# Four layers of cross-attention and feed-forward: next keys behind the routing's choice, ternary weights fetched a region earlier, and a token-major feed-forward 3 with two chunks convolved on TensorE

## The chip, the cores and the metric

The kernel runs on one core of one Trainium2 chip. A core has five engines that run their own instruction streams side by side and wait for each other by semaphores: TensorE (PE, matrix multiply; its weight loads are listed as PEld), VectorE (DVE), ScalarE (ACT), GpSimd (POOL) and SyncE (SP, here a queue for DMAs). The metric is the device time of one execution in microseconds (us); lower is better.

## The reference, cut to what matters

The input is 8 sequences of 256 tokens of 256 values (2048 tokens). Each of four layers adds a gated cross-attention to a context of 256 tokens (16 heads of 16 values) and a gated feed-forward:

```python
for l in range(4):
    x = x + tanh(g_xattn[l]) * xattn[l](layernorm(x), ctx, ...)
    x = x + tanh(g_ffn[l]) * ffn[l](layernorm(x), ...)
```

Feed-forwards 1 and 2 route each token to the best two of eight experts (`top_k(logits, 2)`, then a softmax of the two weights). Feed-forward 3, in which most of the change lies, is:

```python
def act_quant(x):
    scale = 127.0 / clip(max(abs(x), axis=-1, keepdims=True), 1e-05)
    return clip(round(x * scale), -128, 127) / scale
def weight_quant(w):
    scale = 1.0 / clip(mean(abs(w)), 1e-05)
    return clip(round(w * scale), -1, 1) / scale
def bit_linear(x, w):
    return einsum('bsd,hd->bsh', act_quant(x), weight_quant(w))
h = bit_linear(x, w1)                   # 256 -> 1024
h = depthwise_conv1d(h, conv_w, conv_b) # 3 taps along the sequence
h = silu(h)
return bit_linear(h, w2)                # 1024 -> 256
```

So a token's 1024 hidden values need one common maximum before they are rounded, while the convolution runs over neighbouring tokens.

## The kernel before

Tokens lie in 16 tiles of 128 partitions; one batch element is two tiles. The work is emitted as "units", one for each head of each element (16 to an element), with hand-written offsets: `plan(at, f)` puts a piece of work behind unit `at`. Scores run 17 units ahead of the exponentials. A scheduler then orders the instructions of each engine; what goes through `pin` (all matmuls and turns, the exponentials) keeps the order in which it was written.

There are three regions with stages between them. Region 1 is attention 0 and 1 with feed-forward 0 and the routing of feed-forward 1; then the experts of feed-forward 1; region 2 is attention 2 with the routing of feed-forward 2; then its experts; region 3 is attention 3, with feed-forward 3 of an element following its attention.

An attention job projects queries, keys and values by TensorE (pq, pk, pv). `stack` splits queries or keys in three bf16 parts on POOL or DVE (L199 to L204), writes them to DRAM (L281) and reads them back as a stack on 112 partitions (L288), so that one bf16 matmul pair makes a head's scores (sc). DVE takes their negative maximum (L479), a second pair makes the transposed scores (st), ACT exponentiates (L523), `po` multiplies by the values; the turned sums (acc, DVE `o` L555, pm, ACT oT L571) go through py into x (L579).

`tail` puts the first work of the next region into the end of the current one: `early` holds `setup` (loads and the bias matmuls pgb) and keys and values of the next two jobs. Routing (`block`) of four tiles runs as norm, normT (pt_f), out (plf), choose and weigh on DVE, rank (two matmuls), place (DVE builds one-hot tables), tabulate (tabf). `slots` reads the table (tot, tok) and makes indices for indirect DMAs on POOL's queue; these gather tokens (xg) and expert weights (we) for 39 token tiles (L1036). Each tile is turned (ptg), multiplied (phg, gelu L1105, yg), scaled (ysb L1118) and written to yd. Later the `added` pieces of the next region gather the results and add them to x (L1158).

Feed-forward 3 takes two tiles at a time, hidden-major: partitions are hidden units, so eight chunks of 128x256 make up an element. `norm` normalizes (L169 is the power on POOL, L177) and scales by 127 over the maximum (L1248 to L1258), rounding by adding and subtracting the constant RND = 12582912. `normT` turns it on TensorE, and DVE takes RND off (L1264). `hidden(g)` makes two chunks: matmuls ph_f, DVE's multiplication by the scales into hp (L1284), the first tap with bias on ACT (L1294), the third on ACT into z (L1299), the second by DVE (L1301), and z's addition on POOL (L1306); the last element does taps two and three on DVE. Silu is one ACT instruction over 128x2048 (L1309). `largest` reduces the chunks per token on DVE with a strided view (L1316), `over` turns these maxima (pmx) to reduce over partitions, `spread` broadcasts the scales by TensorE (bc_yb) and ACT (L1338), `quantize(g)` multiplies and clips on POOL (L1343, L1344) and rounds on DVE (L1345). `out_` multiplies (y_f) and adds to x (L1357). Its weights are fetched in full precision (f3raw, 1 MB each, L1193) at the start of the second expert stage, summed (L1200) at its steps 8 and 16 and made ternary in quarters (L1220 to L1222).

Of the kernel before, what the change touches and what calls it, by code (L numbers as in the profile page):

```python
# [16 lines left out]
P = 128  # L17
# [21 lines left out]
def kernel(ctx: ExitStack, tc: tile.TileContext, a: dict, out: bass.AP):  # L39
# [183 lines left out]
    def attention(layers):  # L223
# [10 lines left out]
        def setup(l):  # L234
            y = lay[l] = {"bq": None, "bk": None}
            for n in "qkvo":
                w = awpool.tile([P, DC, D], F32, tag=f"w{n}", name=f"w{n}{l}")
                nc.sync.dma_start(w, a[f"L{l}_w{n}"].rearrange("(c p) o -> p c o", p=P))
                y[n] = w
            bv = None  # L240
            if l in (1, 3):
                y["bq"] = load(f"bq{l}", [P, DC], a[f"L{l}_bq"])
                nc.vector.tensor_scalar(y["bq"], y["bq"], 1.0 / DK**0.5, None, ALU.mult)
                y["bk"] = load(f"bk{l}", [P, DC], a[f"L{l}_bk"])
                bv = load(f"bv{l}", [P, DC], a[f"L{l}_bv"])


            bo = row(f"L{l}_bo")
            pb = bank(ps_m, "m", f"pgb{l}")[:, :D]
            if bv is not None:  # L250
                for c in range(DC):
                    bvb = keep.tile([P, P], F32, tag="bvb", name=f"bvb{l}_{c}", bufs=2)
                    nc.vector.tensor_copy(bvb, bv[:, c : c + 1].to_broadcast([P, P]))
                    mm(pb, bvb, y["o"][:, c, :], c == 0, False)
            mm(pb, ones[0:1, :], bo, bv is None, True)
            y["gb"] = keep.tile([P, D], F32, tag="gb", name=f"gb{l}")
            nc.vector.tensor_scalar(y["gb"], pb, tg[:, l : l + 1], None, ALU.mult)
# [38 lines left out]
        def prep(j, l, b):  # L296
# [96 lines left out]
            def proj(s, oc):  # L393

                if oc == 0:
                    o["p"] = bank(ps_m, "m", f"p{s}_{n}").rearrange("p (c s) -> p c s", c=DC)
                    o["t"] = keep.tile([P, DC, S], F32, tag=f"{s}T", name=f"{s}T_{n}")
                src = o["xs"] if s == "q" else ctxT[b]
                for c in range(DC):
                    mm(  # L400
                        o["p"][:, oc, :], lay[l][s][:, c, oc * P : (oc + 1) * P], src[:, c, :],
                        c == 0, c == DC - 1,
                    )
                bias = lay[l][f"b{s}"]
                scale = 1.0 / DK**0.5 if s == "q" else 1.0
                dst = o["t"][:, oc, :]
                if bias is not None:
                    nc.scalar.activation(  # L408
                        dst, o["p"][:, oc, :], AF.Identity, bias=bias[:, oc : oc + 1], scale=scale
                    )  # L410
                elif s == "q":
                    nc.scalar.mul(dst, o["p"][:, oc, :], scale)
                else:
                    nc.scalar.copy(dst, o["p"][:, oc, :])
                if s == "q" and lead and j == 0:

                    o["qs"] = stack(o["t"], s, j, oc, nc.vector)
                elif oc:
                    o[f"{s}s"] = stack(
                        o["t"], s, j, engine=nc.vector if s == "q" and lead and j == 1 else None  # L420
                    )
# [181 lines left out]
        for j, (l, b) in enumerate(jobs):  # L603
            if l and b == 0:
                if j:
                    plan(NH * (j - 2) - AHEAD - 6, setup, l)
                else:
                    early.append(lambda l=l: setup(l))
# [162 lines left out]
    def routing(l, pool, xd, gate, at0):  # L771
# [22 lines left out]
        def block(blk):  # L794
# [140 lines left out]
            def tabulate(h):  # L935
# [15 lines left out]
                (at + 22, out), (at + 23, choose), (at + 26, weigh), (at + 30, rank),  # L951
                (at + 32, lambda: place(0)), (at + 36, lambda: tabulate(0)),
                (at + 37, lambda: place(1)), (at + 41, lambda: tabulate(1)),
# [216 lines left out]
    def ffn3(home):  # L1170

        nh = 8
        w = {}
# [4 lines left out]
        def load_weights():  # L1178
            w["cw"] = load("cw", [P, nh, 3], a["L3_ffn_conv_w"])
            w["cb"] = load("cb", [P, nh], a["L3_ffn_conv_b"])  # L1180

        def ternary(n, at):
# [43 lines left out]
            return [(0, fetch), (at, total), (at + 1, mean)] + [  # L1226
# [13 lines left out]
        def element(pool, b):  # L1240
            n, o = f"f3_{b}", {}
            tiles = [2 * b, 2 * b + 1]

            def norm():

                xn = o["xn"] = normed(tiles, n)
# [7 lines left out]
                for i in range(2):  # L1254
                    nc.vector.tensor_scalar(
                        xn[:, i, :], xn[:, i, :], qs[:, i : i + 1], 127.0, ALU.mult, ALU.min
                    )
                nc.vector.tensor_scalar(xn, xn, -128.0, RND, ALU.max, ALU.add)  # L1258
                o["y"] = hbuf(f"h_{n}")
                o["q"] = pool.tile([P, nh, S], BF16, tag="f3qy", name=f"qy_{n}")  # L1260

            def normT():
                o["xqT"] = pool.tile([P, DC, S], BF16, tag="f3xT", name=f"xqT_{n}")
                nc.vector.tensor_scalar(  # L1264
                    o["xqT"], turn_pair(o["xn"], n), RND, None, ALU.subtract
                )
# [3 lines left out]
            def hidden(g):  # L1270
# [9 lines left out]

                hp = pool.tile([P, 2, S + 2], F32, tag="f3hp", name=f"hp_{n}_{g}")
                nc.gpsimd.memset(hp[:, :, 0:1], 0.0)
                nc.gpsimd.memset(hp[:, :, S + 1 : S + 2], 0.0)
                nc.vector.tensor_tensor(  # L1284
                    hp[:, :, 1 : S + 1], ph, o["dq"].to_broadcast([P, 2, S]), ALU.mult
                )
                cw = w["cw"]
                last = b == B - 1
                if not last:
                    z = pool.tile([P, 2, S], F32, tag="f3z", name=f"z_{n}_{g}", bufs=1)  # L1290
                for k in range(2):
# [6 lines left out]
                    if not last:  # L1298
                        nc.scalar.mul(z[:, k, :], hp[:, k, 2:], cw[:, hc, 2:3])  # L1299
                    for t in (1, 2) if last else (1,):  # L1300
# [3 lines left out]
                if not last:  # L1304
                    y = o["y"][:, 2 * g : 2 * g + 2, :]
                    nc.gpsimd.tensor_tensor(y, y, z, ALU.add)  # L1306

            def silu():
                pin(nc.scalar.activation(o["y"], o["y"], AF.Silu))  # L1309

            def largest():

                mx = pool.tile([P, S], F32, tag="f3mx", name=f"mx_{n}", bufs=1)
                pt = bank(ps_m, "m", f"pmx_{n}")[:, :S].rearrange("p (i s) -> p i s", i=2)
                for i in range(2):
                    nc.vector.tensor_reduce(  # L1316
                        mx[:, i * P : (i + 1) * P],
                        o["y"][:, :, i * P : (i + 1) * P].rearrange("p h s -> p s h"),
                        AX.X, ALU.max, apply_absolute_value=True,
                    )  # L1320
                o["mx"], o["pt"] = mx, pt

            def over():

                mx, pt = o["mx"], o["pt"]
                for i in range(2):
                    turn(pt[:, i, :], mx[:, i * P : (i + 1) * P], ident)
                ym = o["ym"] = small.tile([P, 2], F32, tag="ym", name=f"ym_{n}")
                nc.vector.tensor_reduce(ym, pt, AX.X, ALU.max)
# [6 lines left out]
            def spread():  # L1336
                o["yb"] = pool.tile([P, 1, S], F32, tag="f3yb", name=f"yb_{n}")
                nc.scalar.copy(o["yb"][:, 0, :], across(o["ysc"], f"yb_{n}"))  # L1338

            def quantize(g):  # L1340
                y = o["y"][:, 2 * g : 2 * g + 2, :]
                e = nc.vector if b == B - 1 and g % 2 else nc.gpsimd
                e.tensor_tensor(y, y, o["yb"].to_broadcast([P, 2, S]), ALU.mult)  # L1343
                e.tensor_scalar(y, y, 127.0, -128.0, ALU.min, ALU.max)  # L1344
                nc.vector.tensor_scalar(  # L1345
                    o["q"][:, 2 * g : 2 * g + 2, :], y, RND, RND, ALU.add, ALU.subtract
                )

            def out_(i):
# [14 lines left out]
                (12, norm), (15, normT), (31, silu), (33, largest), (35, over), (37, spread),  # L1364
            ]
            for g in range(nh // 2):
                plan += [
                    (17 + 2 * g, lambda g=g: hidden(g)), (39 + 2 * g, lambda g=g: quantize(g))
                ]
            plan += [(48 + i, lambda i=i: out_(i)) for i in range(2)]  # L1370
# [5 lines left out]
        return [(0, load_weights)] + ternary(1, 8) + ternary(2, 16), pieces  # L1376

    def moe(l, nh, nsets, apart, w, xd, between=(), scale=None):
        with tc.tile_pool(name=f"c{l}", bufs=1) as pool:
            with tc.tile_pool(name=f"rt{l}", bufs=1) as tmp:  # L1380
                rows = slots(l, pool, tmp, w, nsets)
            with tc.tile_pool(name=f"f{l}", bufs=1) as tiles:
# [4 lines left out]
    def tail(early, end):  # L1387

        at = [11, 12, 13, 14, 15, 23, 24, 25, 26]
# [7 lines left out]
    ahead = moe(1, 8, 3, True, w, xd[0])  # L1397
    early, run3 = attention((3,))
    with tc.tile_pool(name="r2", bufs=2) as pool:
        w, pieces = routing(2, pool, xd[1], tg[:, 6:7], 0)  # L1400
        run2(pool, pieces + tail(early, NH * B), ahead)
    with tc.tile_pool(name="f3w", bufs=1) as home:
        weights, pieces = ffn3(home)
        ahead = moe(2, 4, 5, False, w, xd[1], weights, w["nw"])
        with tc.tile_pool(name="r3", bufs=2) as pool:
            run3(pool, pieces(pool), ahead)
# [88 lines left out]
```

## Time and profile before

| what | value |
|---|---|
| runs | 1820.37 us median of 3 (1815.41 to 1821.47) |
| the profiled execution | 1816.64 us, of which the span is 1814.8 |
| mean granted TensorE clock | 0.898 |
| POOL busy | 679.9 us, 37% |
| region 1 | 0 to about 597 us |
| routing end and experts 1 | to about 922 us |
| region 2 | about 925 to 1190 us |
| routing end and experts 2 | to about 1390 us |
| region 3 with feed-forward 3 | 1390 to 1814.8 us |

The borders are read from the chain of work that ended last (the last `py` of a region, the last `ysb` or `yd` of an expert stage). In a group row the columns are line, engine, operation, output and input with their shapes, count, busy us and mean ns of one, then the engine's idle time before them. In a chain row they are the start, the length, the engine (or DMA), tensor and line, and how many instructions the piece holds. A float32 matmul is listed as two records, a turn as one. The groups of feed-forward 3 between 1475 and 1765 us that cost most outside TensorE:

```profile
L1306 POOL TENSOR_TENSOR h_f<-h_f,z_f 128x512 f32<-128x512 f32 x28 | 36.5, 1305 | 83.8 <-DVE h_f L1301 28.9 <-ACT pT L523 20.0 <-DVE ysc_f L1332 15.4
L1301 DVE SCALAR_TENSOR_TENSOR h_f<-hp_f,cw,h_f 128x256 f32<-128x256 f32 x56 | 35.0, 624 | 4.1 <-ACT h_f L1294 3.3
L1343 POOL TENSOR_TENSOR h_f<-h_f,yb_f 128x512 f32<-128x512 f32 x24 | 31.9, 1347 | 1.2 <-ACT yb_f L1338 0.4
L1316 DVE TENSOR_REDUCE mx_f<-h_f 128x128 f32<-128x1024 f32 x12 | 22.7, 1918 | 0.7 <-ACT h_f L1309 0.7
```

### The profile page before, as it was taken

To read this page: it belongs to the slowest core of one execution; us is meant where nothing else is said; L and a number is where in the kernel's file an instruction comes from. 1 tells how busy PE (TensorE), PEld (TensorE's weight loads), DVE (VectorE), ACT (ScalarE), POOL (GpSimd) and SP (SyncE) were. 2 spreads that over 40 slices of the span, in tenths; PEclk is the share of its full clock that TensorE was granted. 3 is DMA by queue.
4 is the path that set the end of the run, shared out by engine and by line. 5 is a ranking of instruction groups with operands and counts; after the bars stand their busy time and mean duration, and the time that the engine had idled before them with its cause. 6 is when DMAs were issued, how large, how long until landed. Compare 5 with 4: busy or idle time off the path is not lost.

```text
span 1814.8 us, 27468 instructions
## 1 busy us (share of the span) xinstructions
PE 1446.9 (80%) x9888; PEld 1097.3 (60%) x9918; DVE 946.7 (52%) x2918; ACT 742.2 (41%) x1629; POOL 679.9 (37%) x816
## 2 busy tenths in 40 slices
PE   1689888999998599999957888866997587776653
PEld 1356666676665399999944555546996454454432
DVE  4655554444767511111137767752422767778777
ACT  0354544555556133333314544512231256555641
POOL 2352232232330244343334453014553445554452
PEclk9899999999999799999978988977998788888876
DMA  6654222222541444242224535027341444222000
GB/s 165 150 152 99 69 60 59 60 60 59 129 131 30 112 150 138 88 135 85 85 71 111 132 96 140 17 78 244 99 149 56 129 100 102 66 56 57 7 6 18
DMA packets 101116, 170.11 MB, mean 94 GB/s; under 512 B 26642, under 2 KB 85141, under 8 KB 90197
## 3 DMA queue, kind: packets, MB, share of 16 engines
q1 hardware_dynamic: 71759, 113.93, 25.7%
q0 software_dynamic: 23664, 52.81, 8.9%
q10 hardware_dynamic: 5558, 1.63, 0.4%
q8 instruction: 78, 1.28, 0.3%
q14 instruction: 57, 0.47, 0.1%
HBM read 224.69 MB, written 41.68 MB: 147 GB/s over the span
## 4 chain that ended last, share of the span: by engine, by line
PE 59%; DVE 20%; DMA 8%; POOL 5%; issue 4%; ACT 3%; SPq 1%; ACTq 0%; POOLq 0%; DVEq 0%
PE phg L192 11%; PE yg L192 11%; PE po L192 5%; PE y_f L192 4%; PE st L192 4%; PE ph_f L192 4%; PE sc L192 4%; PE pv L192 3%; PE pk L192 3%; DVE nm L479 3%; PE pq L192 3%; DMA qstack<-mt 2%; DVE ms L474 2%; DMA kstack<-dr_k_None 1%; DMA xg<-xd,toki 1%
## 5 line engine op out<-in xcount | busy, mean ns | idle before, releaser
L523 ACT ACTIVATE pT<-st 128x512 f32<-128x512 f32 x512 | 298.9, 597 | 286.7 <-PE st L192 244.8
L479 DVE TENSOR_REDUCE nm<-sc 128x2 f32<-128x512 f32 x384 | 256.9, 681 | 119.7 <-PE sc L192 118.7
L192 PE MATMUL sc<-kstack,qstack 112*128 112x256 bf16 x1024 | 213.1, 297 | 95.5 <-DMA kstack<-dr_k_None 28.1
L1105 ACT ACTIVATE hg<-phg,we 128x128 f32<-128x128 f32 x468 | 133.5, 368 | 283.9 <-issue 259.6
L192 PE MATMUL st<-qstack,kstack 115*128 115x256 bf16 x1024 | 210.2, 290 | 44.3 <-ACT pT L523 23.6
L192 PEld LDWEIGHTS phg<-xgT,we 128*128 128x128 f32 x1872 | 224.3, 195 | 7.2 <-DVE xgT L1087 1.8
L192 PE MATMUL phg<-xgT,we 128*128 128x128 f32 x1872 | 225.8, 278 | 2.1 <-DVE xgT L1085 1.0
L192 PE MATMUL yg<-we,hg 128*128 128x256 f32 x936 | 214.6, 380 | 0.0
L192 PEld LDWEIGHTS <-qstack 112*128 112x128 bf16 x1024 | 101.7, 106 | 160.1 <-issue 120.9
L192 PEld LDWEIGHTS yg<-we,hg 128*128 128x128 f32 x936 | 172.2, 191 | 20.0
L192 PE MATMUL po<-pT,va 128*32 128x256 f32 x2048 | 155.0, 422 | 0.9
L192 PEld LDWEIGHTS <-kstack 115*128 115x128 bf16 x1024 | 105.0, 103 | 71.1 <-issue 37.3
L474 DVE CUSTOM_DVE_ANT_0 ms<-sc,mb 128x256 f32<-128x256 f32 x256 | 107.2, 419 | 70.2 <-PE sc L192 60.2
L1118 DVE TENSOR_TENSOR ysb<-yg,we 128x256 f32<-128x256 f32 x78 | 33.0, 424 | 169.3 <-PE yg L192 163.6
L169 POOL TENSOR_TENSOR rsr_ff<-rsv_ff,nhalf 128x4 f32<-128x4 f32 (+2 forms) x24 | 24.4, 1017 | 237.5 <-DVE rsv_ff L167 129.4
L192 PEld LDWEIGHTS po<-pT,va 128*32 128x32 f32 x2048 | 57.6, 117 | 64.3 <-issue 42.1
L1085 DVE COPY xgT<-ptg 128x256 f32<-128x256 f32 x39 | 16.5, 424 | 140.0 <-PE ptg L197 140.0
L1036 POOL DMA_INDIRECT xg<-xd,toki x78 | 74.7, 958 | 24.0 <-issue 23.2
L1036 POOL DMA_INDIRECT yg<-yd,rt_si x64 | 63.0, 984 | 51.4 <-issue 29.9
L1036 POOL DMA_INDIRECT we<-in_L_ffn_wa,wrow x39 | 38.8, 996 | 85.5 <-ACT hg L1105 73.0
L192 PE MATMUL ph_f<-xT_f,f0w 128*128 128x256 f32 x288 | 67.1, 390 | 2.8 <-DVE nm L479 2.0
L192 PE MATMUL pv<-wv,ctxT 128*128 128x256 f32 x192 | 59.7, 439 | 12.0 <-ACT kT L408 7.4
(254 smaller groups left out, 2516.3 us busy)
## 6 DMA issues: line engine op xcount, KB each, us to landing
kstack<-dr_k_None SPq DMA_DIRECT2D x160, 128.0 KB
qstack<-dr_q_None SPq DMA_DIRECT2D x60, 256.0 KB
dr_k_None<-pc_k SPq DMA_DIRECT2D x32, 384.0 KB
dr_q_None<-pc_q SPq DMA_DIRECT2D x30, 384.0 KB
qstack<-dr_q_None SPq DMA_DIRECT2D x30, 384.0 KB
yd<-ysb SPq DMA_DIRECT2D x78, 128.0 KB
kstack<-dr_k_None SPq DMA_DIRECT2D x32, 256.0 KB
xd<-fxn_f SPq DMA_DIRECT2D x8, 512.0 KB
```

The source lines that it names most:

```text
L169: pw = nc.gpsimd.tensor_tensor(rs, ve, nhalf[:, :k, :n], ALU.pow)
L192: pin(nc.tensor.matmul(out, lhsT=lhsT, rhs=rhs, start=start, stop=stop, skip_group_check=True))
L474: nc.vector.tensor_tensor_reduce(masked, sc[:, i, :], o["bias"][:, i, :], -1.0, 3.0e38, ALU.add, ALU.min, o["nm"][:, i, h : h + 1],)
L479: nm = nc.vector.tensor_reduce(o["nm"][:, :, h], sc, AX.X, ALU.max, negate=True)
L523: pin(nc.scalar.activation(pT[u], st, AF.Exp))
L1036: return nc.gpsimd.indirect_dma_start(out=dst, out_offset=None, in_=src, in_offset=bass.IndirectOffsetOnAxis(ap=rows, axis=0), **kw,)
L1085: nc.vector.tensor_copy(xT, pv)
L1105: nc.scalar.activation(h[:, hc, :], ph[:, k, :], AF.Gelu, bias=w[:, n1 - nh + hc : n1 - nh + hc + 1],)
L1118: nc.vector.tensor_tensor(ys, py, w[:, nh * D :], ALU.add)
```

## The change

**Tails.** `setup` keeps its loads; the bias matmuls become `bias`. In the tail only `setup`, `bias` and one job's keys and values remain, keys in two halves; the other job's run after `slots`, in the expert stage. Both jobs' key stacks of a later region are split on DVE.

**Routing.** The pieces from weigh on stand earlier by 2 to 7 units.

**Fetch.** The two 1 MB loads are planned in region 2, at the start of its seventh element. Sums, means and quarters keep their steps in the plan of the second expert stage.

**Feed-forward 3.** The statistics stand two units ahead of the norm; one DVE operation scales and adds RND, ACT takes RND off. hp has two fixed buffers. Chunks 0 and 1 are convolved on TensorE by three diagonal matrices each, and ACT evicts them with the bias. For the other chunks ACT does the first tap and DVE the other two. The chunks are then turned to token-major, ACT does silu while evicting, the maximum is a reduction along the row, and its scale a value per partition; DVE scales and adds RND, TensorE turns back, ACT takes RND off while evicting to bf16. Clipping is gone, as the scale bounds the values.

```diff
         def bias(l):
+            y = lay[l]
+            bo, bv = y["bo"], y["bv"]
             pb = bank(ps_m, "m", f"pgb{l}")[:, :D]
...
-                        o["t"], s, j, engine=nc.vector if s == "q" and lead and j == 1 else None
+                        o["t"], s, j, engine=nc.vector if lead and j == 1 else None
...
-                (at + 22, out), (at + 23, choose), (at + 26, weigh), (at + 30, rank),
-                (at + 32, lambda: place(0)), (at + 36, lambda: tabulate(0)),
-                (at + 37, lambda: place(1)), (at + 41, lambda: tabulate(1)),
+                (at + 22, out), (at + 23, choose), (at + 24, weigh), (at + 27, rank),
+                (at + 28, lambda: place(0)), (at + 31, lambda: tabulate(0)),
+                (at + 31, lambda: place(1)), (at + 34, lambda: tabulate(1)),
...
+            w["hp"] = [home.tile([P, 2, S + 2], F32, tag=f"f3hp{k}", name=f"hp_{k}") for k in range(2)]
...
+                        nc.vector.tensor_scalar(
+                            d[:, k, t, :], ident, cw[:, 2 * g + k, t : t + 1], None, ALU.mult
+                        )
...
-                nc.vector.tensor_scalar(xn, xn, -128.0, RND, ALU.max, ALU.add)
...
+            def whole(dst, src):
+                nc.scalar.activation(dst, src, AF.Identity, bias=w["nrnd"])
...
-                    if not last:
-                        nc.scalar.mul(z[:, k, :], hp[:, k, 2:], cw[:, hc, 2:3])
-                    for t in (1, 2) if last else (1,):
+                    for t in (1, 2):
                         nc.vector.scalar_tensor_tensor(
                             y, hp[:, k, t : t + S], cw[:, hc, t : t + 1], y, ALU.mult, ALU.add
                         )
-                if not last:
-                    y = o["y"][:, 2 * g : 2 * g + 2, :]
-                    nc.gpsimd.tensor_tensor(y, y, z, ALU.add)
+            def convolve(g):
...
+                        mm(
+                            pc[:, k, :], w["tap", g][:, k, t, :], hp[:, k, t : t + S],
+                            t == 0, t == 2,
+                        )
...
             def silu():
-                pin(nc.scalar.activation(o["y"], o["y"], AF.Silu))
+                for i in range(2):
+                    for h in range(2):
+                        py = bank(ps_m, "m", f"yt_{n}_{i}_{h}")
+                        for k in range(4):
+                            turn(
+                                py[:, k * P : (k + 1) * P],
+                                o["y"][:, 4 * h + k, i * P : (i + 1) * P], ident,
+                            )
+                        pin(nc.scalar.activation(
+                            o["yt"][:, i, h * BLK : (h + 1) * BLK], py, AF.Silu
+                        ))
...
-            def quantize(g):
-                y = o["y"][:, 2 * g : 2 * g + 2, :]
-                e = nc.vector if b == B - 1 and g % 2 else nc.gpsimd
-                e.tensor_tensor(y, y, o["yb"].to_broadcast([P, 2, S]), ALU.mult)
-                e.tensor_scalar(y, y, 127.0, -128.0, ALU.min, ALU.max)
+            def quantize(i):
+                y = o["yt"][:, i, :]
+                nc.vector.tensor_scalar(y, y, o["ysc"][:, i : i + 1], RND, ALU.mult, ALU.add)
+
+            def back(i, h):
...
+                    turn(pq[:, k * P : (k + 1) * P], o["yt"][:, i, hc * P : (hc + 1) * P], ident)
...
-                (12, norm), (15, normT), (31, silu), (33, largest), (35, over), (37, spread),
+                (11, measure), (13, norm), (15, normT), (31, silu), (33, largest),
+                (35, lambda: quantize(0)), (36, lambda: quantize(1)),
...
-            plan += [(48 + i, lambda i=i: out_(i)) for i in range(2)]
+            plan += [(37 + k, lambda k=k: back(*divmod(k, 2))) for k in range(4)]
+            plan += [(42 + i, lambda i=i: out_(i)) for i in range(2)]
...
                 rows = slots(l, pool, tmp, w, nsets)
+                for f in early:
+                    f()
...
-        at = [11, 12, 13, 14, 15, 23, 24, 25, 26]
+        at = [11, 24, 23, 24, 34, 38]
...
+            pieces += [(NH * (B - 2), f) for f in fetches]
```

## Prediction

> **What bounds the kernel now.** Four rows of the page come first: the engine sums, and the busy tenths of the span's 40 slices (45.4 us each).
>
> ```profile
> PE 1446.9 (80%) x9888; PEld 1097.3 (60%) x9918; DVE 946.7 (52%) x2918; ACT 742.2 (41%) x1629; POOL 679.9 (37%) x816
> PE   1689888999998599999957888866997587776653
> DVE  4655554444767511111137767752422767778777
> PEclk9899999999999799999978988977998788888876
> ```
>
> TensorE is full only in the expert stages (slices 15 to 20 and 27 to 30). From slice 33 on, which is attention layer 3 with feed-forward 3, neither PE nor DVE is full and the granted clock sinks. The window table says so in us (engine, busy, instructions; then clock):
>
> ```profile
> core 0: us, PE busy (x) PEld busy (x) DVE busy (x) ACT busy (x) POOL busy (x), PEclk, DMA share, GB/s
> 1300.00:1390.00 90.00, 89.72 (x618) 84.26 (x617) 24.78 (x63) 27.44 (x96) 40.49 (x42) 1.00 0.34 107
> 1420.00:1765.00 345.00, 244.35 (x1664) 160.46 (x1663) 262.13 (x581) 191.92 (x364) 169.64 (x227) 0.84 0.26 63
> 1765.00:1815.00 50.00, 17.91 (x84) 11.11 (x84) 36.69 (x65) 7.39 (x12) 14.20 (x17) 0.64 0.05 16
> ```
>
> The experts are pure TensorE. Region 3 (1420 to 1765) has PE 71%, DVE 76%, POOL 49% at clock 0.84: waits passed from engine to engine bound it. The chain of waits through one element (start, length, what) shows them:
>
> ```profile
> 1556.14 2.32 DVE x L1158 x2
> ...
> 1564.75 1.76 POOL x L373 x2
> ...
> 1568.39 0.71 POOL rsr_ff L169
> ...
> 1572.60 1.10 PE pt_f L197 x4
> ...
> 1594.35 0.59 PE acc L197 x4
> ...
> 1595.87 2.51 POOL h_f L1343 x2
> 1598.45 0.62 POOL h_f L1344
> ...
> 1603.62 2.32 DVE x L1158 x2
> ```
>
> Equal points lie 1603.62 − 1556.14 = **47.5 us** apart: one element. The PE pieces of this chain and of the ones beside it, taken where they run at full clock (sc and st 0.22 a pair, po 1.00, py, pk, pv and pq about 2.0, ph_f and y_f 1.76), add up to 27.2 us an element. The wait view gives PE 12.5 us idle in 1556 to 1603: 3.1 for the norm (DVE L1258, which waited for POOL's power L169, itself queued behind L373), 2.8 for DVE `o`, because DVE stood at L1345 waiting for POOL's quantize, 2.3 for ACT, 1.7 for kT, the rest small. The remaining 7.8 us is the half-rate clock after idle: four turns cost 1.10 us at 1572.6 and 0.59 at 1594.
>
> The routing tail, here tail 2, by the chain:
>
> ```profile
> 1205.61 0.66 PE pt_f L197 x4
> 1206.27 1.95 PE plf L192 x16
> ...
> 1211.50 1.72 PE pv L192 x4
> ...
> 1214.80 0.38 PE rankf L192 x4
> ...
> 1226.64 0.62 POOL we L1036
> ...
> 1228.04 10.49 DMA xg<-xd,toki
> ```
>
> Keys and values of the next region stand on PE ahead of `plf` and of `rank`; the first gather then takes 10.49 us (4.75 in tail 1, chain at 630.27), with the two 1 MB ternary weights in front.
>
> **Feed-forward 3, one element.** POOL loses L1306 (4 × 1.31), L1343 (4 × 1.35), L1344 (4 × 0.68) and 8 memsets of 0.1: 14.1 us, at once or by contention. DVE loses 8 L1301 of 0.62 (5.0), 2 L1316 of 1.92 (3.8), 4 L1345 of 0.66 (2.6), L1264 (0.69), L1258 (0.43); it gains 12 STTs (0.48, the median of all L1301: 5.8), two reduces over 128x1024 (half of L1200's 2.28: 1.14 each) and two in-place scalings of 1024 (twice L1221's 0.42: 0.83 each). L1255 stays. −12.5 + 9.7 = −2.8 us. Besides, L1158 takes 1.16 us each beside POOL's quantize and 0.47 to 0.5 elsewhere (0.50 at 932.6), so −1.3. ACT loses 8 z of 0.50, two first terms of 0.59, the 1.91 silu and the 0.38 copy (7.5) and gains 4 silus, 4 evictions and xqT at about 0.59 and two 128x256 evictions at about 0.4 (6.1): −1.4; the table load stays one pair an element in after's order.
>
> PE gains six float32 taps of 128x256 at 0.5 (py: two such in 1.0 to 1.13) = 3.0, and 32 turns; it loses bc_yb 0.46 and pmx 0.22. The acc row of the chain, four turns in 0.59, gives 0.15 a turn: 4.8 us. Against the change speaks the Trainium skill, "TensorE: Matmul & The Clock Gate", Part 4: a turn took about 275 ns in a kernel, and turns don't count as PE work for the clock. By that rule 32 turns are 8.8 us, 4.0 an element or 25 over 6.2 elements more. The trace has both prices, 1.10/4 = 0.275 after an idle and 0.15 in a busy stream; the new turns come in two groups of 16 inside region 3's stream, so I take the 0.15 and keep the 0.275 for the range. PE: 27.2 − 0.7 + 7.8 = **34.3 us**.
>
> Idle: `measure` two steps ahead takes the power off the path (−3.1), no quantize on POOL (−2.8), shorter adds (about −1.5 of 2.3): 12.5 becomes 5.1. New: the first turn for the silu waits for ACT's and DVE's last chunk, and `back` for the DVE scaling: 1 to 2 us, less when other units fill it; I take 1.5. The 7.8 of slow clock should fall with the idle to about 2. Sum 34.3 + 5.1 + 1.5 + 2 ≈ **43 us**, −4.5. What is late next is DVE (36.35 − 4.1 ≈ 32 of 43) and nm L479 behind the scaling. Bounds: 39.5 (idle falls to 4, clock recovers) and 47.5. The feed-forward runs from 1475 to 1765, 290/47 = 6.2 periods: **−28 us** (−50 to 0).
>
> The last element's end, 1793.7 to 1814.8, is 21.1 us: silu 1.9, maxima 3.7, spread 3, POOL 3.4, DVE, y_f. After: 16 turns with 4 silus behind them 4.5, two maxima 2.3, small ones 0.9, two scalings 1.6 partly beside turns, turns and evictions 3, y_f and add 2: 14.3. **−7** (−4 to −9).
>
> **Routing tails.** After's order on PE is pt_f, plf, half of pk, pgb, the other half, rank; later the table matmuls, one v, and only then tot and tok. In tail 2 plf at 1206.27 stands behind 11.2 us of PE (pgb, pk, pv from 1193.95), but its operand is ready only about 1199: plf at 1200 to 1202, choose (3.7 in tail 2, 1208.2 to 1211.9) to 1205.7, while PE does pk and pgb for 2.0 + 3.2 + 2.1 us: rank at about 1209.3 in place of 1214.80, −5.5. The first block's earlier rank and place bring 1, the v ahead of the token matmuls costs 2.2 (full clock) to 3.6 (half), 3 taken: first gather 3.5 us earlier. The other job's k and v and its k stack now fall among the gathers. The stack's DMAs fill all engines for 6.3 us (0.38 MB written, 0.9 MB read); by "DMA: Bandwidth & Descriptors" of the skill (arbitration) an engine alternates between queue rows, so a gather of 4.75 us is at most doubled, while by the row 10.49 it waits for all that is ahead. I take +3, bounds 0 and +6. The ternary fetch gone from there is worth 10.49 − 4.75 = −5.7. Tail 2: −3.5 + 3 − 5.7 ≈ **−6** (−3 to −11). Tail 1, at a faster clock: rank from 616.66 to about 610.5, first block −1, v +3, so −4 for the gathers; the k stack +5, since all three first tiles came at 420 GB/s and landed at 646.8, with no fetch to take away: **+1** (−4 to +3).
>
> **The fetch in region 2.** Planned at unit 96, it has no predecessor, and after's instruction order has both 1 MB loads on SP at region 2's very start, six tap builds (128x128, about 0.3) on DVE before the first adds, and the two totals of 2.28 us inside the first query split. Queued behind a total: pc_q, dr_q, the query stack, the first scores (949.13). Loads: 2 MB at the 420 GB/s of the gathers of tail 1 are 5 us, at 925 to 931, beside the yg gathers (landed 932.5): +1.5 (0 to +4). Totals 4.6, of which DVE's idle before (it waited 2.09 for pq) covers 2.5; taps lie in the wait for yd: **+3** together (0 to +7). Means and quarters are DVE work under a full PE, as before.
>
> Sum against the profiled execution (1816.6; span 1814.8): −28 − 7 − 6 + 1 + 3 = −37, **1780 us**. The median of the three runs shown lies 4 us above that execution, inside their own spread of 6; I leave it out.
>
> **Rivals.**
> - Given back (0.19): DMA at the two entries costs its upper bounds (+7, +3, tail 2 −3) and the period only falls to 44.5: 1816.6 − 19 + 7 + 3 − 3 − 7 ≈ 1798. For: tail 2's 10.49. Against: tail 1's third tile landed only at 646.8 anyway.
> - More (0.14): POOL's absence speeds all DVE rows (L1301 mean 0.66, median 0.48), period 39.5: 1816.6 − 50 − 7 − 6 + 4 ≈ 1757.
> - Slower (0.10): TensorE bounds region 3. Its 7.1 us more an element come on top of idles that only move, with turns at half rate. The rest of the change gives 9 us, 1.5 a period, so it decides from the point where less than 5.6 of the 20.3 us idle and slow clock go away. If 3 go: 51.6 a period, 4.1 × 6.2 = +25, −9: 1833. For: PE's pieces grow by a quarter and clock is 0.84. Against: 5.9 of the idle has a named cause that is removed.
> - No effect (0.05): the same mechanism at about 5.6 us: 1817.
>
> The likeliest (0.52) is 1766 to 1793 by itself. The range, 1745 to 1807, leaves out the slower case and the tail of the fast one. About 0.3% (5 us) is what a measurement tells from no change: faster 0.85, within 0.05, slower 0.10.
>
> **What would show it.** POOL nearly empty in region 3 but for splits, powers and adds; L1158's successor near 0.5 us; period 43 with PE busy above 80% and clock near 0.9; turns 0.15 each; rank right after choose, gathers of tail 2 some 3.5 us earlier; first scores of region 2 about 3 us later; a first gather of tail 2 well under 10.49. It is wrong if PE's idle for DVE stays near 12 us, or if the turns run in 0.275.

## The result and the profile after

The changed kernel takes 1795.9 us (median of 4, 1787.15 to 1800.92) where the kernel before took 1819.11; the ratio is 0.9877, 95% interval 0.9847 to 0.9908. It is faster by 1.2%, inside the forecast's range, by about 23 us instead of 37. The same rows of the page, and the window table over region 3 up to the last attention output, and from there to the end:

```profile
PE 1483.7 (83%) x10192; PEld 1135.7 (63%) x10222; DVE 911.7 (51%) x2913; ACT 742.5 (41%) x1629; POOL 573.0 (32%) x660
PE   1589988999999689999966887876999378888876
DVE  4655554454667611111117678754332557766865
PEclk9799999999999799999986999877999689888998
```

```profile
core 0: us, PE busy (x) PEld busy (x) DVE busy (x) ACT busy (x) POOL busy (x), PEclk, DMA share, GB/s
1420.00:1755.00 335.00, 269.68 (x1923) 189.58 (x1924) 232.56 (x578) 186.36 (x351) 85.80 (x99) 0.90 0.27 67
1755.00:1794.00 39.00, 25.11 (x148) 18.60 (x145) 22.32 (x53) 14.78 (x26) 0.70 (x1) 0.86 0.06 21
```

POOL has lost half its work in region 3 (170 to 86 us), DVE 30 us, TensorE has gained 25 us, and its clock went from 0.84 to 0.90. That is the forecast's picture. But a sum hides what happened. The table below cuts the span of each profile at the same events, read from the timelines: the last attention output added to x in a region (py), the first token matmul (tok), a tile's first turn (ptg), the last ysb, and the fourth gathered result added (yg). Each entry is the time since the row above, in us. The last three columns are experiments told below.

| up to | before | changed | feed-forward 3 alone | tails alone | values behind slots |
|---|---|---|---|---|---|
| last py, region 1 | 600.5 | 598.0 | 597.5 | 603.8 | 596.7 |
| tok, tail 1 | 25.5 | 29.7 | 25.6 | 29.9 | 25.7 |
| third tile's ptg | 20.9 | 23.1 | 21.0 | 22.8 | 22.3 |
| last ysb, experts 1 | 275.6 | 275.6 | 275.6 | 276.1 | 277.3 |
| fourth yg | 10.5 | 13.0 | 12.9 | 9.8 | 13.4 |
| last py, region 2 | 258.6 | 256.9 | 259.1 | 255.0 | 255.6 |
| tok, tail 2 | 32.5 | 33.9 | 31.9 | 34.2 | 30.0 |
| first tile's ptg | 14.5 | 9.1 | 8.9 | 9.1 | 9.6 |
| last ysb, experts 2 | 151.5 | 155.2 | 150.4 | 168.0 | 152.2 |
| fourth yg | 10.0 | 9.9 | 9.8 | 9.9 | 9.9 |
| py of element 0, region 3 | 80.5 | 82.6 | 80.1 | 80.6 | 79.8 |
| py of element 3 | 131.2 | 130.0 | 125.0 | 130.7 | 127.8 |
| py of element 7 | 152.7 | 138.3 | 138.7 | 152.7 | 137.3 |
| end | 50.3 | 39.1 | 38.3 | 50.4 | 38.3 |

Region 3 (the last four rows) fell from 414.7 to 390.0 us; everything ahead of it rose by 4.4. The forecast had −35 and −2. A row holds one execution of each kernel: region 1, which the change hardly touches, differs by 2.5 us. In both tails the token matmul, which was to come about 4 us earlier, came later. The chain of waits in tail 1 of the changed kernel shows how:

```profile
600.48 1.41 PE pt_f L197 x8
601.91 3.38 PE plf L192 x16
605.30 1.91 PE pk L192 x4
607.20 1.15 PE pgb L192 x2
608.35 2.02 PE pk L192 x4
...
610.90 0.56 DVE rt_c L892
611.67 1.02 DVE rtf_run L878
...
619.55 0.52 PE tabf L192 x2
620.07 1.83 PE pv L192 x4
621.92 0.38 ACT va L435
622.34 2.07 PE pv L192 x4
624.42 0.24 PE tot L192 x2
```

`plf` starts 5.0 us earlier than before (606.91), of which 2.5 are region 1's, and the gain is lost step by step. TensorE was idle for 3.0 us until 600.48 and has a granted clock of 0.52 from there to 636: plf takes 3.38 us where it took 1.95. Then DVE's choose takes from 605.3 to 614.6 where it took 3.7: it holds an instruction that waits for pgb (1.52 us of idle in the DVE timeline) and weigh's first step, which waits for ACT's exponential (1.03). Two of the four run sums L878 take 1.10 and 1.13 us for 8 values each while POOL splits a key stack. (The change moved only the second job's key stack to DVE, at 633.27; the first job's is still split on POOL, from 610.83.) Last, both halves of a value projection and an eviction between them, 4.3 us, stand between the last table and `tot`. In tail 2 rank does come early, 18.2 us behind the last py in place of 23.1; there two DVE steps behind it take 1.17 us each beside POOL's split (0.17 and 0.34 otherwise), and the value with its eviction takes 4.2.

In region 3 the chain of the element from 1569 to 1617 us shows another loss:

```profile
1574.97 0.94 PE pq L192 x4
...
1576.49 1.28 ACT L1358
1577.78 0.61 ACT yt_f L1358
...
1578.43 1.13 PE yt_f L197 x4
...
1579.58 0.61 ACT yt_f L1358
...
1580.23 1.13 PE yt_f L197 x4
...
1581.38 0.61 ACT yt_f L1358
...
1582.03 1.13 PE yt_f L197 x4
...
1583.83 1.13 PE pt_f L197 x4
```

The four groups of turns ahead of the silu and the four evictions go strictly one after the other. ACT's 1.28 us at 1576.49 load the silu's table. Three of the groups take 1.13 us: 0.28 a turn, the price of the half-rate clock (0.50 granted from 1578.4 to 1592). The PSUM pool has two banks, but half of the query projection stands at 1574.97 and its second half comes only behind the turns, so its bank stays open and the turns have one. Behind the silu ACT also evicts the next element's norm before it loads the table of the exponentials again:

```profile
1576.49 1.28 ACT L1358 ACT_TABLE_LOAD   x1
1587.37 1.28 ACT L527 ACT_TABLE_LOAD   x1
```

So 10.9 us pass from one load to the other without an exponential; in the same place of the kernel before they are 6.1 (1570.04 to 1576.12).

### The profile page after: what moved, and what is told of

It is laid out like the page before. It is cut to its first block, busy times and chain, and to the rows that moved or that the text cites. A ratio compares the mean times of both kernels' runs of the same rounds, so it can differ in the third digit from the quotient of the medians.

```text
span 1794.6 us, 27891 instructions
## 1 busy us (share of the span) xinstructions
PE 1483.7 (83%) x10192; PEld 1135.7 (63%) x10222; DVE 911.7 (51%) x2913; ACT 742.5 (41%) x1629; POOL 573.0 (32%) x660
## 4 chain that ended last, share of the span: by engine, by line
PE 58%; DVE 18%; issue 8%; DMA 7%; POOL 4%; ACT 3%; SPq 0%; POOLq 0%; ACTq 0%; DVEq 0%
PE yg L192 11%; PE phg L192 11%; PE po L192 5%; PE ph_f L192 4%; PE y_f L192 4%; PE st L192 4%; PE sc L192 4%; DVE nm L483 3%; PE pk L192 3%; PE pq L192 2%; PE pv L192 2%; DMA xg<-xd,toki 2%; DMA kstack<-dr_k_None 2%; DVE ms L478 1%; DMA qstack<-mt 1%
## 5 line engine op out<-in xcount | busy, mean ns | idle before, releaser
L192 PE MATMUL sc<-kstack,qstack 112*128 112x256 bf16 x1024 | 208.8, 292 | 100.2 <-DMA kstack<-dr_k_None 32.2
L192 PE MATMUL st<-qstack,kstack 115*128 115x256 bf16 x1024 | 205.2, 284 | 19.2 <-DMA qstack<-mt 15.7
L192 PE MATMUL po<-pT,va 128*32 128x256 f32 x2048 | 150.8, 416 | 0.9
L169 POOL TENSOR_TENSOR rsr_ff<-rsv_ff,nhalf 128x4 f32<-128x4 f32 (+2 forms) x24 | 24.4, 1015 | 327.5 <-DVE rsv_ff L163 188.0
L1041 POOL DMA_INDIRECT yg<-yd,rt_si x64 | 63.4, 991 | 51.4 <-issue 29.7
L169 POOL TENSOR_TENSOR rsr_a<-rsv_a,nhalf 128x2 f32<-128x2 f32 x32 | 23.5, 738 | 147.2 <-DVE rsv_a L163 146.8
L192 PE MATMUL pq<-xs,wq 128*128 128x256 f32 x192 | 65.3, 472 | 4.4 <-ACT qT L412 1.9
```

Of the source, the lines that this page charges most:

```text
L169: pw = nc.gpsimd.tensor_tensor(rs, ve, nhalf[:, :k, :n], ALU.pow)
L192: pin(nc.tensor.matmul(out, lhsT=lhsT, rhs=rhs, start=start, stop=stop, skip_group_check=True))
L1041: return nc.gpsimd.indirect_dma_start(out=dst, out_offset=None, in_=src, in_offset=bass.IndirectOffsetOnAxis(ap=rows, axis=0), **kw,)
```

## The experiments

**Feed-forward 3 alone.** The changed kernel with the tails, the routing offsets and the fetch's planned place of before:

```diff
-                (at + 22, out), (at + 23, choose), (at + 24, weigh), (at + 27, rank),
+                (at + 22, out), (at + 23, choose), (at + 26, weigh), (at + 30, rank),
...
-        at = [11, 24, 23, 24, 34, 38]
+        at = [11, 11, 12, 13, 14, 15, 23, 24, 25, 26]
...
-    ahead = moe(1, 8, 3, True, w, xd[0], early[6:])
+    ahead = moe(1, 8, 3, True, w, xd[0], [])
...
```

> Feed-forward 3 of the changed kernel alone; tails, routing offsets and the fetch as before. Theory A (region 3 gains about 25 us, the entries of regions 2 and 3 together give back about 4): 1794 less 4, about 1790 us, with first x addition of region 3 at 1399.6 as before and about 24 us less from there to the end. Rival B (the tails and the fetch help, as forecast, by about 12 us in the full change): 1805 us or more.

Measured: 1776.28 us, ratio 0.9772 (0.9721 to 0.9822), below even theory A. Region 3 falls by 32.6 us (table), and the yg gathers and the first tile of the second experts come as in the changed kernel, since the loads still went out at region 2's start (see below). Of the 40.0 us between the two profiles 3.0 lie in region 1, which feed-forward 3 doesn't touch.

**Tails alone**, on the kernel before: the split of setup, the routing offsets, the new places, the second job's keys and values behind the slots and its key stack on DVE.

> Tails and routing offsets of the changed kernel alone; fetch and feed-forward 3 as before. Theory A (value projections ahead of the token matmuls and key stacks among the gathers cost more than the earlier rank brings): slower than before by 4 to 10 us, last ysb of the first experts at about 926 in place of 922.2. Rival B (the forecast's sum of the tails without the fetch, +1 and about 0): within 2 us of before.

Measured: 1840.07 us, ratio 1.0115 (1.0072 to 1.0158): slower by 20 us, twice theory A's upper end. The changed kernel lies 19.6 us above feed-forward 3 alone, so the tails cost about 20 us in both surroundings, though not in the same places: the second experts take 168.0 us here, 16.5 more than before, and in the changed kernel 4.8 more than with feed-forward 3 alone. The wait view of TensorE in that stage (us in total, times, longest), and DVE's timeline there (in brackets the idle time and its cause):

```profile
PE phg L192 <- DVE xgT L1093: 9.1, 3, 8.4
PE yg L192 <- DVE ysb L1124: 3.1, 1, 3.1
PE phg L192 <- issue: 3.0, 1, 3.0
```

```profile
1260.75 2.29 DVE L1206 TENSOR_REDUCE wab<-f3raw 128x1 f32<-128x2048 f32 x1 [8.98 <-DMA f3raw<-in_L_ffn_w]
1262.95 0.41 DVE L1093 TENSOR_TENSOR xgT<-ptg,nw 128x256 f32<-128x256 f32 x1
```

DVE's sum over the first raw weight waits 9 us for its load, whose issue on SP (1241.77) stands behind the second job's key stack, and the next tile's eviction (xgT) stands behind the sum.

**Fetch put back**, in the changed kernel's plan.

```diff
-            fetches.append(fetch)
-            return [(at, total), (at + 1, mean)] + [
+            return [(0, fetch), (at, total), (at + 1, mean)] + [
```

> The changed kernel with the two 1 MB ternary loads put back at the start of the second expert stage. Theory A (the loads at region 2's start cost there 5 to 6 us, through the yg gathers and two totals, of which most is hidden later by region 2's slack; in tail 2 they cost about 5.7): between 0 and 6 us slower than the changed kernel, first scores of region 2 at about 951 and first gathered tile of the second experts some 5 us later. Rival B (the early loads only cost): faster than the changed kernel by 4 us or more.

Measured: 1802.17 us (1786.2 to 1806.92), 0.99 (0.9854 to 0.9946), not separable from the changed kernel. And its edit moved nothing: SP issues both loads at 929.03, against 929.19 in the changed kernel. The load waits for no one, so it goes out where its buffers exist, and they are opened before region 2. What moves the fetch is the pool, not the plan. Neither theory was tested. The version serves as a second measurement of practically the same instruction order: its median lies 6.3 us from the changed kernel's and its region 3 takes 382.7 us in place of 390.0, elements 1 to 3 of it 125.2 in place of 130.0. Smaller differences between two medians or two profiles show nothing by themselves.

**Fetch really late**: feed-forward 3 alone, with the pool opened behind region 2 (loads at 1208.58 and 1212.04).

```diff
-    with tc.tile_pool(name="f3w", bufs=1) as home:
-        fetches, weights, pieces3 = ffn3(home)
-        with tc.tile_pool(name="r2", bufs=2) as pool:
+    with tc.tile_pool(name="r2", bufs=2) as pool:
...
+    with tc.tile_pool(name="f3w", bufs=1) as home:
+        fetches, weights, pieces3 = ffn3(home)
```

> Feed-forward 3 alone, its buffers opened only behind region 2, so that the two ternary loads go out with the second experts' first gathers as before. Theory A (the early loads cost about 2.5 us at the yg gathers of region 2 and save about 5.5 before the second experts' first tile): 2 to 5 us above feed-forward 3 alone, first tile of the second experts 14.5 us behind the token matmul in place of 9. Rival B (the place of the loads does not matter once slack is counted): within 1 us.

Measured: 1782.81 us (1772.02 to 1786.4), against 1776.28 (1773.42 to 1784.5): the ranges overlap. In the profile the fourth yg came after 10.7 us in place of 12.9, the first tile of the second experts after 13.6 in place of 8.9: −2.2 and +4.7, as theory A has them, though the total doesn't prove it. (Tails alone reach 9.1 us at that first tile too, without an early fetch: their loads stand behind the key stack on SP and go out at 1241.77, behind the first gathers, where the kernel before has them at 1220.79.)

**Tails alone with the early pool**, to see what the fetch does for the tails.

> Tails and routing offsets alone, with the ternary buffers opened before region 2, so that the two 1 MB loads go out at its start. Theory A (in the tails-alone kernel DVE's sum over the first raw weight waits for a load queued behind the second job's key stack, and holds the next tile's turn for TensorE): the waits of 8.4 and 3 us in the second experts go, that stage takes 152 to 160 us in place of 168, 1825 us. Rival B (the key stacks' own DMAs make the stage long): within 4 us of tails alone, 1840.

Measured: 1833.51 us (1824.68 to 1841.66, 15 runs), 1.0071 (1.005 to 1.0092). The second experts take 156.9 us in place of 168.0, as theory A had it. The total fell by less, 6.6 us; against tails alone in the profile, yg took 3.0 us and region 2 another 7.4 us more (region 2 differs by as much among the other profiles). So the early fetch repairs the stall in the experts that the tails make, and the tails stay slower than before.

**Values behind the slots**: the changed kernel, with the last two places taken out of the tail.

```diff
-        at = [11, 24, 23, 24, 34, 38]
+        at = [11, 24, 23, 24]
...
-    ahead = moe(1, 8, 3, True, w, xd[0], early[6:])
+    ahead = moe(1, 8, 3, True, w, xd[0], early[4:])
...
```

> The changed kernel with both value projections of the first job taken out of the tail too and placed behind the slots, with the second job's. Theory A (each tail loses the 4.2 us that two value halves stand ahead of the token matmuls): first token matmul 25.5 us after the last py of region 1 in place of 29.7, the same in tail 2, 5 to 9 us faster than the changed kernel, about 1788 us. Rival B (the key stacks' DMAs decide when the third tile lands): within 3 us of the changed kernel.

Measured: 1777.78 us (1777.3 to 1785.64), 0.9779 (0.9735 to 0.9823): 18 us below the changed kernel, with intervals apart. The token matmuls come 4.0 and 3.9 us earlier, as theory A says; the second experts take 3.0 us less; the rest is spread over region 2's end and region 3 in the two single profiles, and what carries it there isn't settled. This one placement is the cost of the new tails: without it they equal the old ones (1776.28). The rows name 11 of its 18 us.

**Silu one unit later**, behind the second half of the query projection, with all that follows it; first in the changed kernel, then in feed-forward 3 alone.

```diff
-                (11, measure), (13, norm), (15, normT), (31, silu), (33, largest),
-                (35, lambda: quantize(0)), (36, lambda: quantize(1)),
+                (11, measure), (13, norm), (15, normT), (32, silu), (34, largest),
+                (36, lambda: quantize(0)), (37, lambda: quantize(1)),
...
```

> The changed kernel with silu and all pieces behind it one unit later, so that the query projection has closed its PSUM bank before the turns. Theory A (the four groups of turns go through one bank, one after the other, because the other is held open by a half-done query projection): in the three elements concerned the waits of yt for ACT fall from 3.5 us to under 1.5 and the elements get 3 to 5 us shorter, 9 to 14 us in all: about 1784 us. Rival B (the turns wait for ACT anyway, or DVE decides): within 3 us of the changed kernel.

> Feed-forward 3 alone (tails and routing as before), with silu and what follows one unit later. Theory A (free second PSUM bank for the turns): 5 to 10 us below feed-forward 3 alone, 1766 to 1771 us. Rival B (the gain of the first such run lies in the tails): within 3 us of feed-forward 3 alone, 1776.

Measured: 1790.99 us, 4.9 below the changed kernel, and 1771.54, 4.7 below feed-forward 3 alone; each pair's ranges overlap, and two measurements of one order lay 6.3 us apart, so the totals alone don't show a gain; both go the same way by the same amount. One element of feed-forward 3 alone, first as it is, then with the later silu, each in its window and its wait of the turns for ACT (us in total, times, longest):

```profile
1551.00:1597.00 46.00, 37.47 (x263) 26.49 (x261) 31.45 (x82) 26.28 (x49) 13.48 (x17) 0.89 0.31 76
```

```profile
PE yt_f L197 <- ACT yt_f L1357: 3.5, 3, 2.1
```

```profile
1556.00:1597.00 41.00, 34.38 (x265) 24.74 (x265) 31.64 (x82) 25.88 (x49) 14.29 (x17) 1.00 0.33 85
```

```profile
PE yt_f L197 <- ACT yt_f L1357: 1.3, 1, 1.3
```

The wait falls to 1.3 us and the granted clock rises to 1.00, as theory A says; elements 1 to 3 take 116.6 us in place of 125.0. With the early silu they took 125.0 to 130.0 in five profiles, with the late one 116.6 and 120.4, so this gain stands. Whether the free bank alone makes it isn't shown, because the edit also moves the silu behind the next element's norm, whose evictions stood between the silu and the exponentials. The two table loads of this element now lie 3.7 us apart:

```profile
1567.48 1.28 ACT L1357 ACT_TABLE_LOAD   x1
1571.22 1.28 ACT L527 ACT_TABLE_LOAD   x1
```

But the last stretch grows from 38.3 to 40.8, and the sum stays below what was expected: behind the last attention a later silu is only late.

**No convolution on TensorE**, feed-forward 3 alone.

```diff
-        TAPS = (0,), (0,)
+        TAPS = (), ()
```

> Feed-forward 3 alone with no chunk convolved on TensorE: all eight chunks go through ACT and two DVE operations. Theory A (DVE and ACT are nearer the limit than TensorE): 3 to 10 us above feed-forward 3 alone, mostly in the last element. Rival B (TensorE is the bound, the six taps of 0.5 us cost 3 us an element): 5 to 15 us below it.

Measured: 1765.07 us (1757.35 to 1774.74), 0.9704 (0.9647 to 0.9761), 11 us below feed-forward 3 alone, as rival B says, though the intervals overlap (0.9721 was the other's lower end). The gain is 3.1 us in elements 1 to 3, 8.9 in 4 to 7 and 4.4 at the end. The second of these elements, 1597 to 1641 us with taps and 1597 to 1637 without:

```profile
1597.00:1641.00 44.00, 36.55 (x266) 26.27 (x265) 30.12 (x74) 26.39 (x49) 9.94 (x12) 0.92 0.28 67
```

```profile
1597.00:1637.00 40.00, 30.97 (x247) 21.81 (x246) 32.62 (x77) 26.11 (x49) 9.48 (x11) 1.00 0.32 74
```

TensorE works 5.6 us less, of which the taps are about 3 and the rest goes with the higher clock; DVE works 2.5 more, and the element is 4 us shorter.

**Combinations.** Both edits on feed-forward 3 alone; both on the whole change with values behind the slots; and the last with the keys behind rank, the bias later and weigh planned behind rank (`at = [11, 35, 28, 30]`, weigh at 29).

> Feed-forward 3 alone on the tails and routing of before, without the TensorE convolution and with silu one unit later. Theory A (both gains are TensorE time and add up: 11 and 5 us below 1776): about 1760 us. Rival B (without taps the silu's bank matters less): 1765 us, as without taps alone.

> The whole changed kernel with value projections behind the slots, no TensorE convolution and silu one unit later. Theory A (the same two gains on top of 1778): about 1762 us, equal to the version with the old tails within 4 us. Rival B (key stacks among the gathers still cost): 5 us or more above it.

> As the last, and in the tail the first job's keys behind rank instead of ahead of it, the bias behind the keys, weigh planned behind rank. Theory A (rank waited for two key halves and the bias, choose for the bias and for the softmax's exponential): token matmul 21 to 23 us behind the last py in place of 25.6, in both tails, so about 6 us below the last: 1755 us. Rival B (half-rate clock eats it): within 3 us of the last.

Measured: 1780.35 us (0.9775, 0.9734 to 0.9816), 1776.02 (0.9755, 0.9709 to 0.9802) and 1786.68 (0.9816, 0.9772 to 0.986). The gains don't add up, and without the taps the later silu's version is 8.8 us slower than with them (1771.54). The kernel before took 1820.1 us on the chip of one of these two and 1821.4 on that of the other, so the chip is hardly the reason. With the later silu the version without taps takes 138.0 us for elements 4 to 7 and 40.9 at the end, where it had 129.8 and 33.9; in elements 1 to 3 it gains nothing in this profile (122.4 against 121.9), though the next version, with the same code there, took 117.6. Elements 1 to 7 of four versions: feed-forward 3 alone, the same without taps, with the later silu, and with both:

```profile
1472.80:1736.50 263.70, 215.41 (x1586) 152.87 (x1584) 187.78 (x475) 158.54 (x297) 53.13 (x62) 0.93 0.22 53
1474.80:1726.60 251.80, 196.17 (x1502) 136.88 (x1500) 203.96 (x503) 158.93 (x297) 53.84 (x62) 0.93 0.23 56
1479.90:1732.50 252.60, 206.24 (x1586) 145.69 (x1584) 187.70 (x476) 156.97 (x297) 54.39 (x62) 0.98 0.23 56
1474.70:1735.00 260.30, 207.87 (x1500) 144.46 (x1499) 202.80 (x503) 158.83 (x297) 54.91 (x62) 0.88 0.23 54
```

With the early silu the missing taps save 19 us of TensorE and 12 us of time at one clock (0.93). With the later silu TensorE saves nothing, since the clock sinks from 0.98 to 0.88, and 8 us are lost. In the next version, with the same code in the region, the clock was 0.93 and the time 252.5. So what the taps and the second bank are worth together stays open. The third version puts rank right behind choose (613.16 in its chain), but the token matmul comes 25.9 us behind the last py as before: half-rate plf (3.33 us), the two key halves now stand ahead of the tables, and two of DVE's table columns took 1.09 and 1.10 us beside POOL's split (0.26 before). None of the three theories A held in its time; that the two kinds of tail come out nearly alike (4.3 us apart) did. The fastest version measured, by its median, is feed-forward 3 alone without the convolution.

## Why the prediction was right or wrong

**Sign and range** were right, the size off by 16 us. The profiles' spans differ by 20.2 us where 37 were forecast. Against the forecast's parts the elements of region 3 lack 14.5 us and the tails 7.4 (5.4 and 2.0), and the second experts took 3.7 more, for which the forecast had no term; the other way the end brought 4.2 more than forecast and the entry of region 2 2.2, and 2.5 are region 1's, which is luck.

**Region 3** held the largest error: −28 for the elements and −7 for the end. Measured −13.5 and −11.2 in the changed kernel, −20.6 and −12.0 with feed-forward 3 alone, whose code in the region is the same; the version with the fetch put back has the changed kernel's order and takes 382.7 us in region 3, as feed-forward 3 alone does (382.1), so that difference comes from one execution to the next. The step that failed is the period of 43 us. Before, the seven distances between elements are 36.7, 47.1, 47.5, 46.2, 38.9, 35.7 and 31.9 us, since the last elements have no projections of a later job; after, they are 38.2, 44.2, 47.6, 44.6, 34.1, 33.5 and 26.1. The middle ones, from which the period was worked out, lost about 1.5 us each and not 4.5. The waits that the forecast named did shrink: in the element at 1569 the norm's is gone (3.1) and `o`'s is 0.5 (2.8). The mis-sized terms are the new wait and the slow clock, 1.5 and 2 us. ACT's table load and evictions of the silu hold TensorE up for 4.2 us there (3.5 ahead of the turns, 0.7 behind them), and its clock does not recover:

```profile
1569.50:1617.10 47.60, 39.07 (x267) 27.46 (x265) 31.87 (x82) 26.28 (x49) 13.91 (x16) 0.86 0.30 73
```

TensorE's 39.1 us are 4.8 more than the sum's 34.3, and 8.5 us are idle where 6.6 were forecast.

The turns were not mispriced. In region 3 of the changed kernel:

```profile
L197 PE MATMUL yt_f<-ident,h_f 128*128 128x128 f32 x128 | 22.5, 314 | 17.5 <-ACT yt_f L1358 17.2
L197 PE MATMUL qt_f<-ident,yt_f 128*128 128x128 f32 x128 | 21.6, 299 | 11.5 <-ACT qy_f L1294 4.5 <-DVE yt_f L1378 3.4 <-DVE hp L1313 1.8
L197 PE MATMUL yt_f<-ident,h_f x128: 271/273/477, 1529.2 to 1781.6; 128*128 128x128 f32 x128
```

The 256 turns keep TensorE busy for 44.1 us, 0.17 each, so 5.5 us an element where 4.8 were taken. The Trainium skill's 0.275 us ("TensorE: Matmul & The Clock Gate", Part 4) agrees here with the length of one turn's record (median 0.273), but the records overlap, so the 8.8 us that the forecast worked out from it are too many. The chain's 0.28 a turn is the half-rate price; by the spacing of their starts 11 of the 64 groups of four paid it. Whether turns alone keep the full clock no run shows, but they do run at it: eight of them at 1785.28, behind a wait of 3.4 us, took 1.06 us at a granted clock of 1.00.

**The tails** were the other wrong step. The forecast took −5.5 for rank in tail 2, about −6 in tail 1, and +3 for the value ahead of the token matmuls, so 3.5 to 4 us earlier. Measured: 4.2 later in tail 1 and 1.4 later in tail 2. The value's two halves cost 4.3 and 4.2 us, at half rate with an eviction between them. Counted from the last py, rank came 5.0 us earlier in tail 2, as forecast, and then lost half of that, mostly beside POOL's split; in tail 1 it came 0.6 earlier. There the gain was eaten by plf at half rate after the idle that the change itself creates, and by choose, which the forecast took over from the old trace at 3.7 us though the change puts pgb and weigh into it and a POOL split beside it. The term "k stack among the gathers", +5 in tail 1 and +3 in tail 2, came out at +2.2 and, against feed-forward 3 alone, +0.2; the two gathers of tail 1's chain took 4.78 and 10.88 us (4.75 and 8.79 before), far from doubled. What the forecast didn't have is the second experts: +3.7 us with the early fetch, and +16.5 without; the cause of the 3.7 isn't traced.

**The fetch** was right: +3 at region 2's start (measured 2.5 at the yg gathers; region 2 then takes 1.7 us less) and −5.7 ahead of the second experts (−5.4, and −4.7 where the loads alone were moved). That the loads go out at region 2's start whatever their place in the plan was shown by the edit that moved nothing.

**The taps** were costed rightly at 3 us an element of TensorE (24.4 us in all). Whether they help isn't settled: with the early silu the time fell without them, with the late one it did not.

**The rival** "given back" (1798) names the measured time, but not for its reason: the DMAs cost about what was forecast, and TensorE's order in the tails and the elements, which gained less than even its −19, did the rest.

## What to carry to other kernels

When work is moved out of a critical tail, look at what still stands in order between the last dependent step and the next one on the same engine: one projection of 4.3 us there cost the whole benefit. Cost added work by the granted clock that its stage will have: behind the tail's idle sixteen small matmuls took 3.38 us in place of 1.95. A pool of two banks counts as one while a half-finished accumulation holds the other, and ACT's order counts between two table loads. Cut the span at the same events before and after; per-element periods differ, and one of them is no mean. Measure one order twice: here that alone moved region 3 by 7 us.

## What the hardware showed

Small VectorE instructions can last as long as GpSimd's: sums of 128x8 that take 0.16 us took 1.10 and 1.13 in the first tail of the changed kernel, beside GpSimd's 1.15 us over 128x512 (L202 and L204), and ended within 0.03 us of them (612.69 and 612.66, 614.63 and 614.61). In the second tail a scaling of 128x8 took 1.17 in place of 0.17 and a 128x128 table column 1.17 in place of 0.34, with ends 0.03 and 0.08 us behind. A chain of some twenty small steps, as choose is, is therefore a bad neighbour for a split.
